# Deeper gather buffers for a third of the run, and paired column blends, in a deformable convolution with experts

## The chip, the cores and the metric

The kernel runs on one core of a Trainium2 chip. The core has a matrix engine (PE; its weight loads are shown apart as PEld), a vector engine (DVE), a scalar engine (ACT), a GpSimd engine (POOL) and a SyncE queue (SP) that only issues transfers. All transfers run on 16 DMA engines that the queues share. Each engine takes its instructions in the order of its own queue and waits on semaphores for the others. The metric is the device time of one execution in microseconds; the time before is the median of three runs.

## The reference

The input is four images of 256 channels and 64 x 64 positions. Each is normalised over its channels and goes through three modulated deformable 3 x 3 convolutions with ReLU. A plain convolution gives, for each position and each of nine taps, an offset (dy, dx) and a mask; the image is sampled there bilinearly, and the samples are multiplied by the tap's 256 x 256 weights:

```python
om = conv(x, w_off) + b_off                  # 27 channels: 9 x (dy, dx), 9 masks
sampled = _bilinear(x, ys, xs) * mask[:, None]
out = jnp.einsum('bikhw,oik->bohw', sampled, wk) + b[None, :, None, None]
```

The result is added to the input. Then each of the 16384 tokens (256 values) is normalised, a gate picks two of eight experts, and each expert is a layer 256 to 512 with GELU and a layer 512 to 256, weighted by the gate and added. All is float32.

## The kernel before

**Stages and blocks.** The convolution work is cut into twelve stages, one per layer and image, in the order (0,0), (1,0), (0,1), (2,0), (1,1), (0,2), (2,1), (1,2), (0,3), (2,2), (1,3), (2,3), given as (layer, image). The document numbers them 0 to 11. Image 0 leaves its last layer with stage 3; the experts of an image run beside later stages, so the first expert work falls in stage 4. A stage has 8 blocks of 512 positions, a block 9 taps, and a tap 4 tiles of 128 positions: 288 tiles a stage, 3456 in all. Tiles are handled in pairs (`t0` is 0 or 2).

**A tile.** The image lies in DRAM as a table whose row holds a position and the one below it, 512 floats. One gather (POOL, L503) brings for each of 128 positions two neighbouring rows of the table (left and right column), 4 KB, into a buffer `g` of the pool `gat` (ten buffers, 512 KB each). The *column blend* (DVE, L509) mixes the upper and the lower value in each of the two columns, in place, 128 x 512 values. The *row blend* (DVE, L514) mixes the left and the right column into a sample `s` of the pool `smp` (eight buffers), 128 x 256 values; with it the gather's buffer is free. ACT multiplies the sample by its mask (L517). PE transposes the two halves of the sample into `tp` (L532); ACT copies the `tp` of a pair into `sT` (L535); the sample buffers are free after the transposes. When a tap has its two pairs, PE multiplies `sT` by the tap's weights into `acc` (L555): four products of 128 x 512.

**Order.** `samples` puts out a pair's gathers, blends and scalings; `turn` puts out the transposes and copy of the pair that came LAG = 2 pairs earlier; `finish` puts out the products of the tap before. That is the order in the program. A planner then fixes the queue of each engine from a priority, the buffers it believes free and its own estimate of durations, so a change in one engine's order can change another's. Where the code wants an order it says so with `self.after(x)`: what is put out under it comes behind `x` on its engine. `self.last` holds the latest row blend, and the smaller DVE work is put behind it: the plans of positions and weights (`off_block`, L395 to L427, one per block, behind products L357 and L371), the norm of an image to come (`pre_block`), the tokens (`tokens`).

**The experts.** From stage 4 on, lanes paced by the tap counter put out the routing (`route`, `invert`), the expert steps (`expert`: gather of weights and of 256 tokens, transposes `ftp`, copy `fzT`, products `ph` L856, GELU `hT`, products `py` L874) and the weighted sums (`combine`). Their buffers are the pools `ffn`, `rt` and `gyp`, which in the kernel before are there from the start.

## Time and profile before

| what | value |
| --- | --- |
| median of the runs | 7486.86 us (7480.8, 7486.86, 7520.67) |
| profiled execution, its own time | 7520.62 us |
| its span, first to last instruction | 7518.9 us |
| mean granted TensorE clock | 0.944 |
| transfers | 2223.73 MB, mean 296 GB/s |
| of them gathers and other software transfers | 1947.35 MB |

Stretches from the first gather of a stage to that of the next, in us, with busy time of the engines and busy share of DMA:

| stage | from | long | PE | DVE | ACT | POOL | DMA |
| --- | --- | --- | --- | --- | --- | --- | --- |
| 0 | 93.40 | 558.40 | 487.89 | 406.38 | 254.00 | 310.02 | 0.88 |
| 1 | 651.80 | 466.50 | 388.29 | 340.60 | 215.10 | 306.30 | 0.93 |
| 2 | 1118.30 | 478.80 | 411.43 | 347.38 | 226.49 | 307.18 | 0.92 |
| 3 | 1597.10 | 498.00 | 435.22 | 421.44 | 250.57 | 315.71 | 0.96 |
| 4 | 2095.10 | 543.70 | 480.26 | 401.78 | 250.68 | 345.56 | 0.90 |
| 7 | 3820.00 | 634.30 | 533.11 | 422.88 | 266.36 | 407.76 | 0.85 |
| 10 | 5625.30 | 765.80 | 656.77 | 445.31 | 307.43 | 451.10 | 0.78 |

How to read the profile: a group's line gives code line, engine, operation, output and inputs, shapes and count; then busy time and the mean of one in ns; then the idle time of the engine just before these instructions and what ended it. The chain is followed back from the last instruction: at each step to what released it, or to the instruction before it on its engine; only what is on it set the end. A matmul's end is modelled, so PE's busy time holds some waiting. A line of the timeline gives start, length, engine, code line, operation, shapes, how many in a row, and in brackets the idle time before and who ended it.

### The profile page before, as it was taken

Reading aid. Unit: us, or ns where it says so; the run is one execution under the profiler, and the core shown is the slowest. Engines: PE = TensorE matmul, PEld = TensorE weight load, DVE = VectorE, ACT = ScalarE, POOL = GpSimd, SP = SyncE. Lnnn points to the kernel's source line nnn. Section 1 sums busy time; section 2 is a strip of 40 time slices with the busy share of each in tenths; the row PEclk is TensorE's granted clock in tenths of the full one; section 3 lists DMA queues with packets and bytes.
Section 4 is the critical chain, followed back from the end, with each engine's and each line's share of the span. In section 5 each row is a group of like instructions: output and inputs, shape, how many; then the busy total and the mean of one; then the engine's idle time right before and its main releaser. Section 6 shows DMA issues by size and latency. Waiting matters only on the chain.

```text
span 7518.9 us, 88985 instructions
## 1 busy us (share of the span) xinstructions
PE 6443.2 (86%) x26500; PEld 3618.8 (48%) x26500; DVE 4952.9 (66%) x11467; ACT 3266.0 (43%) x7141; POOL 4476.5 (60%) x4245
## 2 busy tenths in 40 slices
PE   6898888888898888889988888888888788977887
PEld 3443333334454444445554445444544555644565
DVE  6776777768887666567777556666768554667421
ACT  3444544445544444445443434444444333444322
POOL 4654666656666565556557656555656565666543
PEclk8999999999999999999999999999999899989998
DMA  8997999989998888888888888888888777888644
GB/s 266 337 325 274 352 342 335 346 331 356 362 349 311 300 305 297 278 315 322 314 293 316 293 280 314 295 302 294 308 306 299 251 271 240 288 302 287 211 139 123
DMA packets 800320, 2223.73 MB, mean 296 GB/s; under 512 B 104729, under 2 KB 302873, under 8 KB 794081
## 3 DMA queue, kind: packets, MB, share of 16 engines
q0 software_dynamic: 551200, 1947.35, 73.3%
q1 hardware_dynamic: 248640, 270.69, 10.9%
q8 instruction: 215, 3.52, 0.2%
q14 instruction: 265, 2.16, 0.1%
HBM read 2160.68 MB, written 196.40 MB: 313 GB/s over the span
## 4 chain that ended last, share of the span: by engine, by line
PE 69%; ACT 10%; issue 7%; another core or an unknown queue 6%; DVE 4%; DMA 2%; POOL 1%; SPq 0%; ACTq 0%; DVEq 0%; POOLq 0%
PE acc L555 34%; PE tp L532 10%; PE ph L856 7%; PE py L874 6%; PE po L357 6%; ACT sT L535 4%; ACT s L517 3%; DVE g L509 2%; DVE s L514 1%; PE pm L371 1%; ACT hT L866 1%; PE ftp L840 1%; ACT win L577 1%; PE tpv L325 1%
## 5 line engine op out<-in xcount | busy, mean ns | idle before, releaser
L503 POOL DMA_INDIRECT g<-tab,idx x3456 | 3685.4, 1066 | 2371.6 <-DVE s L514 1061.8
L555 PE MATMUL acc<-sT,wk 128*128 128x512 f32 x6912 | 3492.1, 620 | 253.4 <-ACT sT L535 147.5
L509 DVE SCALAR_TENSOR_TENSOR g<-g,cf 128x512 f32<-128x512 f32 x3456 | 2559.2, 742 | 269.1 <-DMA g<-tab,idx 245.5
L514 DVE SCALAR_TENSOR_TENSOR s<-g,cf 128x256 f32<-128x256 f32 x3456 | 1662.7, 483 | 1331.3 <-PE tp L532 729.9
L535 ACT COPY sT<-tp 128x512 f32<-128x512 f32 x1728 | 1002.0, 585 | 2312.0 <-PE tp L532 1553.0
L517 ACT ACTIVATE s<-s,cf 128x256 f32<-128x256 f32 x3456 | 1629.5, 508 | 256.7 <-DVE s L514 160.7
L555 PEld LDWEIGHTS acc<-sT,wk 128*128 128x128 f32 x6912 | 1198.9, 198 | 1106.7 <-issue 816.7
L532 PEld LDWEIGHTS tp<-ident,s 128*128 128x128 f32 x6912 | 893.2, 146 | 1666.2 <-issue 898.9
L532 PE MATMUL tp<-ident,s 128*128 128x128 f32 x6912 | 1287.3, 286 | 439.2 <-ACT s L517 253.8
L856 PE MATMUL ph<-fzT,w 128*128 128x256 f32 x2608 | 720.8, 411 | 78.0 <-ACT fzT L844 28.1
L874 PE MATMUL py<-w,hT 128*128 128x256 f32 x2608 | 671.1, 396 | 103.5 <-ACT hT L866 58.0
L856 PEld LDWEIGHTS ph<-fzT,w 128*128 128x128 f32 x2608 | 506.3, 205 | 212.9 <-issue 69.6
L874 PEld LDWEIGHTS py<-w,hT 128*128 128x128 f32 x2608 | 484.5, 196 | 242.0 <-issue 91.9
L866 ACT ACTIVATE hT<-ph,w 128x256 f32<-128x256 f32 x652 | 281.9, 471 | 616.3 <-PE ph L856 378.2
L812 POOL DMA_INDIRECT zt<-z,tok x326 | 333.8, 1024 | 161.5 <-issue 88.0
L800 POOL DMA_INDIRECT w<-in_W,wrow x163 | 178.0, 1092 | 381.2 <-issue 138.8
L357 PE MATMUL po<-win,wo 128*32 128x504 f32 (+1 forms) x2304 | 366.0, 615 | 6.5 <-ACT win L301 4.2
L892 DVE TENSOR_TENSOR y<-py,w 128x512 f32<-128x512 f32 x163 | 111.9, 686 | 341.5 <-PE py L874 285.1
L915 POOL DMA_INDIRECT gy<-ys,slots x256 | 255.6, 998 | 104.5 <-issue 70.0
L930 DVE SCALAR_TENSOR_TENSOR ta<-gy,cw,ta 128x256 f32<-128x256 f32 x256 | 120.6, 480 | 125.6 <-DMA gy<-ys,slots 78.4
L357 PE MATMUL po<-win_pre,wo 128*32 128x504 f32 (+1 forms) x1152 | 184.2, 617 | 2.0 <-ACT om L366 2.0
L366 ACT ACTIVATE om<-po,bo 128x512 f32<-128x512 f32 x96 | 65.9, 687 | 265.3 <-PE po L357 156.3
(154 smaller groups left out, 2961.0 us busy)
## 6 DMA issues: line engine op xcount, KB each, us to landing
tab<-hv SPq DMA_DIRECT2D x512, 128.0 KB
g<-tab,idx POOLq DMA_INDIRECT x3456
ys<-y SPq DMA_DIRECT2D x163, 256.0 KB
tab<-h_pre SPq DMA_DIRECT2D x128, 256.0 KB
wk<-in_conv_w SPq DMA_DIRECT2D x99, 256.0 KB
xc_pre<-in_x SPq DMA_DIRECT2D x32, 512.0 KB
xr_tok<-in_x SPq DMA_DIRECT2D x32, 512.0 KB
t<-t_tok SPq DMA_DIRECT2D x32, 512.0 KB
```

Source lines behind the costliest of these rows:

```text
L357: nc.tensor.matmul(po[g * Q : (g + 1) * Q, :].rearrange("q (r w) -> q r w", w=W)[:, :, x0:x1], lhsT=self.wo[l][:, 3 * ky + kx, c, :], rhs= ...
L503: self.gathered = nc.gpsimd.indirect_dma_start(out=g.rearrange("p x s f -> p (x s f)"), out_offset=None, in_=self.table(*self.stages[i]), ...
L509: nc.vector.scalar_tensor_tensor(g[:, :, 0, :], g[:, :, 1, :], cf[:, j, 0:1], g[:, :, 0, :], ALU.mult, ALU.add,)
L514: self.last = nc.vector.scalar_tensor_tensor(s, g[:, 1, 0, :], cf[:, j, 1:2], g[:, 0, 0, :], ALU.mult, ALU.add)
L517: nc.scalar.activation(s, s, AF.Copy, scale=cf[:, j, 2:3])
L532: self.turned = nc.tensor.transpose(tp[:, c, u * P : (u + 1) * P], ss[u][:, c * P : (c + 1) * P], self.ident)
L535: nc.scalar.copy(self.sT[:, :, t0 * P : (t0 + 2) * P], tp)
L555: nc.tensor.matmul(acc[:, o, :], lhsT=self.wk[k][:, c, o * P : (o + 1) * P], rhs=sT[:, c, :], start=(k == 0 and c == 0), stop=(k == K - 1 ...
L812: self.nc.gpsimd.indirect_dma_start(out=zt, out_offset=None, in_=grp.zd, in_offset=bass.IndirectOffsetOnAxis(ap=grp.tok[:, j : j + 1], axi ...
L856: nc.tensor.matmul(ph[:, h, :], lhsT=w1[:, o : o + P], rhs=zT[:, c, :], start=(c == 0), stop=(c == CC - 1),)
L866: nc.scalar.activation(ht[:, h, :], ph[:, h, :], AF.Gelu, bias=w1[:, k : k + 1])
L874: nc.tensor.matmul(py[:, u, :], lhsT=hT[h // 2][:, h % 2, u * P : (u + 1) * P], rhs=w2[:, h * C : (h + 1) * C], start=(h == 0), stop=(h == ...
```

## The change

For stages 0 to 3 two more pools, `gatx` and `smpx`, of eight buffers each stand beside `gat` and `smp`; gathers and samples go round over 18 and 16 buffers in place of 10 and 8. The pools `ffn`, `rt` and `gyp` are no longer made at the start. When stage 4 begins, `late_pools` gives the two extra pools back, makes the three expert pools in their place, and gathers and samples go on with 10 and 8.

In `samples`, a pair's two column blends now come first and its two row blends after them; `self.after(newest)` holds both row blends behind the second column blend. In the kernel before, each tile's row blend came right after its own column blend.

```diff
--- before.py
+++ after.py
@@ -36,6 +36,8 @@
 FT = 1 << FT_LOG
 FU = FT // P
 GB = 10
+GS = 8
+GX = 8
 LAG = 2
 LEAST = 2.0**-30
 WINN = CC * (RPB + 2) * W
@@ -138,13 +140,19 @@
         self.wt = pool("wt", 2)
         self.small = pool("small", 1)
         self.big = pool("big", 2)
-        self.ffn = pool("ffn", 2)
-        self.rt = pool("rt", 1)
         self.rt2 = pool("rt2", 2)
-        self.gyp = pool("gyp", 4)
         self.smT = pool("smT", 2)
-        self.smp = pool("smp", 8)
+        self.smp = pool("smp", GS)
         self.gat = pool("gat", GB)
+        self.pool = pool
+        self.early = ctx.enter_context(ExitStack())
+        more = [
+            self.early.enter_context(tc.tile_pool(name=name, bufs=GX))
+            for name in ("gatx", "smpx")
+        ]
+        self.gats = [self.gat] * GB + [more[0]] * GX
+        self.smps = [self.smp] * GS + [more[1]] * GX
+        self.drawn = 0
         self.ps = pool("ps", 3, space=bass.MemoryType.PSUM)
         self.ps1 = pool("ps1", 1, space=bass.MemoryType.PSUM)
 
@@ -479,6 +487,14 @@
         )
         self.wk[k] = wk
 
+    def late_pools(self):
+
+        self.early.close()
+        self.gats, self.smps = [self.gat], [self.smp]
+        self.ffn = self.pool("ffn", 2)
+        self.rt = self.pool("rt", 1)
+        self.gyp = self.pool("gyp", 4)
+
     def main_block(self, i, n, wins):
         l, b = self.stages[i]
         plan = self.plans.pop((l, b, n))
@@ -496,24 +512,32 @@
 
         nc = self.nc
         idx, cf = plan
-        ss = []
+        ss, gs = [], []
         for t in (t0, t0 + 1):
             j = t * K + k
-            g = self.gat.tile([P, 2, 2, C], F32, tag="g", name=f"g_{i}_{n}_{j}")
+            g = self.gats[(self.drawn + len(gs)) % len(self.gats)].tile(
+                [P, 2, 2, C], F32, tag="g", name=f"g_{i}_{n}_{j}"
+            )
             self.gathered = nc.gpsimd.indirect_dma_start(
                 out=g.rearrange("p x s f -> p (x s f)"),
                 out_offset=None,
                 in_=self.table(*self.stages[i]),
                 in_offset=bass.IndirectOffsetOnAxis(ap=idx[:, j : j + 1], axis=0),
             )
-            nc.vector.scalar_tensor_tensor(
+            newest = nc.vector.scalar_tensor_tensor(
                 g[:, :, 0, :], g[:, :, 1, :], cf[:, j, 0:1], g[:, :, 0, :],
                 ALU.mult, ALU.add,
             )
-            s = self.smp.tile([P, C], F32, tag="s", name=f"s_{i}_{n}_{j}")
-            self.last = nc.vector.scalar_tensor_tensor(
-                s, g[:, 1, 0, :], cf[:, j, 1:2], g[:, 0, 0, :], ALU.mult, ALU.add
-            )
+            gs.append((j, g))
+        for j, g in gs:
+            s = self.smps[self.drawn % len(self.smps)].tile(
+                [P, C], F32, tag="s", name=f"s_{i}_{n}_{j}"
+            )
+            self.drawn += 1
+            with self.after(newest):
+                self.last = nc.vector.scalar_tensor_tensor(
+                    s, g[:, 1, 0, :], cf[:, j, 1:2], g[:, 0, 0, :], ALU.mult, ALU.add
+                )
             nc.scalar.activation(s, s, AF.Copy, scale=cf[:, j, 2:3])
             ss.append(s)
         return ss
@@ -1071,6 +1095,8 @@
         self.ffn_constants()
         for i, (l, b) in enumerate(self.stages):
             wins, pre = {}, {}
+            if self.stages[i - 1] == (NL - 1, 0):
+                self.late_pools()
             for n in range(NB):
                 for gen in self.later[:2]:
                     self.aside(6, gen, True)
```

## The prediction

> **What bounds the kernel now.** I read the page's busy times and chain first, then the waits of the first four stages (the only ones that get the new buffers), then one tap in the timeline, then the two blends.
>
> ```profile
> PE 6443.2 (86%) x26500; PEld 3618.8 (48%) x26500; DVE 4952.9 (66%) x11467; ACT 3266.0 (43%) x7141; POOL 4476.5 (60%) x4245
> PE 69%; ACT 10%; issue 7%; another core or an unknown queue 6%; DVE 4%; DMA 2%; POOL 1%; SPq 0%; ACTq 0%; DVEq 0%; POOLq 0%
> PE acc L555 34%; PE tp L532 10%; PE ph L856 7%; PE py L874 6%; PE po L357 6%; ACT sT L535 4%; ACT s L517 3%; DVE g L509 2%; DVE s L514 1%; PE pm L371 1%; ACT hT L866 1%; PE ftp L840 1%; ACT win L577 1%; PE tpv L325 1%
> ...
> L509 DVE SCALAR_TENSOR_TENSOR g<-g,cf 128x512 f32<-128x512 f32 x3456 | 2559.2, 742 | 269.1 <-DMA g<-tab,idx 245.5
> L514 DVE SCALAR_TENSOR_TENSOR s<-g,cf 128x256 f32<-128x256 f32 x3456 | 1662.7, 483 | 1331.3 <-PE tp L532 729.9
> ```
>
> PE and the ACT work tied to it make 79% of the chain; VectorE has 4%, DMA and GpSimd 3% together. So a faster VectorE or an earlier gather can shorten only a small part. The waits from 93.4 to 2095 us, where there is no expert work (columns: total us, times, longest):
>
> ```profile
> ACT sT L535 <- PE tp L532: 609.8, 380, 5.7
> ...
> POOL g L503 <- DVE s L514: 292.1, 262, 10.9
> ...
> DVE s L514 <- PE tp L532: 198.0, 252, 4.9
> ...
> ACT s L517 <- DVE s L514: 45.8, 40, 10.4
> ...
> DVE g L509 <- DMA g<-tab,idx: 13.2, 4, 10.9
> ```
>
> The 292 and 198 us are what a lack of buffers looks like: GpSimd waits for a gather buffer, VectorE for a sample buffer that PE has not turned yet. But they are waits of engines that are ahead. VectorE waited for a gather only 13.2 us, and ACT for a sample only 45.8 us, of 2002. What sets the pace there is seen in one tap:
>
> ```profile
> 902.67 0.38 PE L532 MATMUL tp<-ident,s 128*128 128x128 f32 x2
> ...
> 903.14 0.59 ACT L535 COPY sT<-tp 128x512 f32<-128x512 f32 x1 [2.62 <-PE tp L532]
> ...
> 903.62 0.91 ACT L517 ACTIVATE s<-s,cf 128x256 f32<-128x256 f32 x2
> ...
> 904.19 0.83 PE L532 MATMUL tp<-ident,s 128*128 128x128 f32 x4 [0.28 <-ACT s L517]
> ...
> 905.06 0.58 ACT L535 COPY sT<-tp 128x512 f32<-128x512 f32 x1 [0.53 <-PE tp L532]
> ...
> 905.70 1.12 PE L555 MATMUL acc<-sT,wk 128*128 128x512 f32 x2 [0.68 <-ACT sT L535]
> ```
>
> ACT holds the copy of one pair ahead of the scaling of the next, idles 2.62 us for PE, then copies and scales, and PE waits in turn: a loop of PE and ACT. It is set by the order of the two queues. More sample buffers do not let ACT past its copy.
>
> **The change, part by part.** Each number is a change to the profiled execution of 7520.6 us (span 7518.9 and 1.7 around it). That execution lies 33.8 us (0.45%) above the median of the runs shown, 7486.9; the sum is carried to the median unscaled.
>
> *Column blends ahead of row blends.* No instruction is added or removed; the VectorE queue is reordered, the GpSimd queue is the same instruction by instruction, SyncE's has three loads of tokens (ta) later and three others swapped with a neighbour. What VectorE gains is in its timeline, first the old order, then a place where the old kernel already had two columns and two rows together:
>
> ```profile
> 900.47 0.75 DVE L509 SCALAR_TENSOR_TENSOR g<-g,cf 128x512 f32<-128x512 f32 x1
> 901.35 0.48 DVE L514 SCALAR_TENSOR_TENSOR s<-g,cf 128x256 f32<-128x256 f32 x1
> 901.76 0.74 DVE L509 SCALAR_TENSOR_TENSOR g<-g,cf 128x512 f32<-128x512 f32 x1
> ...
> 3940.20 1.41 DVE L509 SCALAR_TENSOR_TENSOR g<-g,cf 128x512 f32<-128x512 f32 x2
> 3941.53 0.88 DVE L514 SCALAR_TENSOR_TENSOR s<-g,cf 128x256 f32<-128x256 f32 x2
> 3942.32 1.41 DVE L509 SCALAR_TENSOR_TENSOR g<-g,cf 128x512 f32<-128x512 f32 x2
> ```
>
> Column to its own row: 901.35-900.47 = 0.88 us from start to start; row to the next column: 0.41. A pair is 2 x 1.29 = 2.58. Together, two columns take 3941.53-3940.20 = 1.33 and two rows 3942.32-3941.53 = 0.79: 2.12 a pair. That is 0.46 x 1728 pairs = 795 us off VectorE's queue.
> How much is on the path? The page gives the two blends 2% and 1% of the chain (1.6% and 1.2% unrounded), 2.8% of 7519 = 210 us. A pair is 2 x (0.742+0.483) = 2.45 us busy, so at most 210 x 0.46/2.45 = 39 us goes, and less where another chain is close behind or where a pair already stands together. Bounds: 0, and all of ACT's idle time before L517 that a blend ended, 160.7 (whole run) + 23.9 = 185 us. I take -30, near the chain's figure, since the chain is the row that weighs a wait by what follows it.
> [...]
>
> *Eight more buffers of each kind, stages 0 to 3.* They take away up to 292 us of GpSimd's and 198 us of VectorE's waiting. Cover: gathers already land about ten tiles early (13.2 us of waiting). If the cover counted for nothing and every wait of ACT for a row blend went, 45.8 us; at the other end 0, or a loss if eighteen gathers in flight press on other transfers (below). Some of the 45.8 is already in the 30 above: I take -10.
> [...]
>
> *PE's order.* The new VectorE order changes what the planner thinks is ready, and it writes another PE queue. Before, a tap's products stood between the transposes of tile one and two; now the two tiles' transposes mostly stand together. That alone is neutral: the second tile's transposes start after the same work. Two counts in the queues matter. (a) Taps whose first product has under 0.85 us of other PE work behind the transposes whose copy it needs (the time from the transposes' issue to the product above): 305 of 864 before, 378 after, 73 more. Waits of this kind, and of the next, over the whole run:
>
> ```profile
> DVE g L509 <- DMA g<-tab,idx: 245.5, 90, 10.9
> ...
> PE acc L555 <- ACT sT L535: 147.5, 171, 5.5
> ...
> PEld ph L856 <- ACT fzT L844: 47.7, 68, 3.4
> ```
>
> 147.5/171 = 0.86 us each, 63 us for 73 as the upper end; many are covered in part, and at the 0.55 us or so that the placement leaves on average I take +40. Lower end 0. (b) First products of an expert step (ph) with under 0.85 us of work behind their own transposes (ftp): 67 of 163 before, 14 after. 47.7/68 = 0.70 us each, 37 us for 53; at 0.5, since PE had other work under part of it, -26. Lower gain 0. The other hops (tile to tile, om to pm) keep their counts within 5 us.
>
> *Waits that the pairing adds.* Row one now waits for column two, so for gather two. VectorE waited for a gather 90 times in the run; behind such a late gather the pair now has column, row, row (0.66+0.40+0.48) in place of column, row (0.88+0.48): 0.2 to 0.3 us more, 27 us if all of it were on the path. Queued behind row one are ACT's scaling of both tiles and PE's transposes, and gather buffer one is freed one column (0.66 us) later. DMA has 2% of the chain: +5, between 0 and 27.
>
> *The pools' change-over before stage 4.* By then the rotation has come round evenly (1152 tiles, over 18 and over 16), so the gathers just fall back to ten ahead. The expert pools' first use is after that; their first three loads on SyncE come some fifty rows later in its queue, long before the sums that need them. 0.
>
> Sum: -30 -10 +40 -26 +5 = **-21 us**, 7466.
>
> **The rivals.**
> *VectorE was the real bound.* For: in stages 3 and 4 (1597 to 2639 us) its blends alone are about 8% of the chain, and the time from a row blend to its transposes often falls to 1.1 us there. If all that ACT waited for blends goes and (b) is full: -185 x 0.5 (half of ACT's waits reaching PE) - 37 = about -130, 7357; the middle of this case, with half of that beside the sum, 7410. Against: elsewhere VectorE is blocked by PE 730 us in total, so it is ahead.
> *PE's order costs more than it gives (the other side).* 73 taps more wait at 0.86, and (b) gains little because expert steps have other waits: +63, with nothing from VectorE +60, 7550. It decides as soon as (a) exceeds the VectorE and expert gains together, 66 us at my figures, so only where one of these fails too.
> *Traffic.* Eighteen gathers of 512 KB ahead in stages 0 to 3, where DMA is already busy 0.88 to 0.96 of the time, delay table stores and what the chain calls an unknown queue (6%, some 490 us). For: that share is large and unexplained. Against: consumption, not issue, sets the rate of gathers. A tenth more of it is +49: 7535.
> *The blends don't speed up* (start to start stays 0.88): only 30 us are lost from the sum, 7496, no change.
>
> **How the numbers follow.** A change under 0.5% (37 us) is about what a measurement of this kernel can't tell from none. No change, the forecast: 0.36, 7466, own range 7450 to 7524. VectorE the bound: 0.34. PE's order: 0.19. Traffic: 0.11. So faster 0.34, same 0.36, slower 0.30. The range takes in the first two rivals to where their bounds add: low -39-46-37 = -122, 7365; high +63+27 = +90, 7577.
>
> **What would show it.** Right: VectorE's start-to-start from column to column 0.66 and its busy time nearly unchanged while its waits grow; POOL g <- DVE s and DVE s <- PE tp far smaller before 2095 us, with stages 1 and 2 still 460 to 485 us each; PE acc <- ACT sT up from 147.5 towards 190; ph <- ACT fzT nearly gone. Wrong: stages 0 to 2 shorter by over 20 us each (the buffers mattered), the DVE share of the chain falling by over 100 us in stages 3 to 11, or the unknown queue's share moving by more than a point.

## The result, and the profile after

The changed kernel takes 7890.8 us (median of 4, 7871.6 to 7958.0), the kernel before 7492.0 (4 runs): **1.053 times as long, 95% interval 1.048 to 1.058**. The forecast was no change, 7466, in a range that ended at 7577. The profiled execution took 7907.3 us (span 7905.6), 386.7 more than the one of before.

Cut at the first transposes of each stage, stages 0 to 3, which have the new buffers, went from 2015.5 to 2385.5 us (+370). Stages 4 to 10, which have the new order with the old buffers, went from 4294.6 to 4287.7. So the whole loss of this execution lies where both parts of the change are present. Within stages 0 to 3, PE idles 303 us more (274 to 577) and is busy 67 us longer (1742 to 1809) for the same work.

From the page of the changed kernel (busy times; chain by engine and by line; the gather and the column blend):

```profile
PE 6503.6 (82%) x26500; PEld 3664.7 (46%) x26500; DVE 4802.0 (61%) x11467; ACT 3255.6 (41%) x7141; POOL 4991.9 (63%) x4245
...
PE 62%; another core or an unknown queue 12%; ACT 10%; issue 8%; DVE 4%; DMA 3%; POOL 2%; SPq 0%; ACTq 0%; POOLq 0%; DVEq 0%
...
L521 POOL DMA_INDIRECT g<-tab,idx x3456 | 4135.4, 1197 | 2267.2 <-DVE s L538 1077.0
...
L527 DVE SCALAR_TENSOR_TENSOR g<-g,cf 128x512 f32<-128x512 f32 x3456 | 2489.2, 743 | 638.6 <-DMA g<-tab,idx 561.9
```

The column blend itself is as long as before (743 ns in the mean, 742 before). What grew is the share of the unknown queue, from 6% to 12% of a longer span, and the gather on GpSimd, from 1066 to 1197 ns in the mean. The waits from 91.4 to 2450 us, the stages 0 to 3 of this run (total us, times, longest):

```profile
POOL g L521 <- DVE s L538: 385.8, 177, 20.0
...
ACT sT L559 <- remote: 219.1, 33, 24.5
...
DVE g L527 <- DMA g<-tab,idx: 99.8, 78, 10.3
...
DVE s L538 <- PE tp L556: 70.3, 47, 4.7
```

VectorE's wait for a sample buffer fell from 198 to 70 us, as the buffers should make it. But GpSimd waits more, not less (292 to 386), VectorE now waits for gathers (13 to 100), and another row has grown: ScalarE's copy waits 219 us for something that the profile calls remote, up to 24.5 us at a time. Before, from 91 to 2095 us, it was:

```profile
ACT sT L535 <- remote: 53.7, 12, 10.6
```

The same 500 us of the two kernels (columns: busy us and instruction count of PE, PEld, DVE, ACT, POOL; then granted PE clock, DMA share, GB/s), before and after:

```profile
600.00:1100.00 500.00, 422.95 (x1688) 190.40 (x1683) 356.92 (x741) 229.01 (x507) 302.82 (x285) 0.97 0.89 321
```

```profile
600.00:1100.00 500.00, 367.07 (x1437) 163.25 (x1434) 284.43 (x652) 187.00 (x416) 288.61 (x229) 0.88 0.75 268
```

Every engine does less in the same time, GpSimd takes longer for each of its instructions (1.26 us of busy time for 1.06), and the granted clock falls from 0.97 to 0.88. The clock record of the run is made of windows at 1.0 and at 0.5; those at 0.5 sum to 166 us in stages 0 to 3 before and to 487 after. PE's work in a window at 0.5 takes longer (an `acc` product 1061 ns in the median there and 592 elsewhere, by the profile's modelled ends), so the 67 us of longer busy time can come from there.

**First finding: gathers are held off.** The changed kernel's timeline around one gather:

```profile
1013.47 16.63 POOL L521 DMA_INDIRECT g<-tab,idx  x1 [0.30 <-issue]
...
1027.88 1.41 DVE L527 SCALAR_TENSOR_TENSOR g<-g,cf 128x512 f32<-128x512 f32 x2
...
1029.70 0.88 DVE L538 SCALAR_TENSOR_TENSOR s<-g,cf 128x256 f32<-128x256 f32 x2 [0.41 <-PE tp L556]
...
1030.41 0.99 POOL L521 DMA_INDIRECT g<-tab,idx  x1 [0.30 <-DVE s L538]
...
1031.70 0.94 POOL L521 DMA_INDIRECT g<-tab,idx  x1 [0.30 <-issue]
```

A gather that usually takes 1 us takes 16.63. VectorE runs columns and rows without any gap all this time; its first gap is from 1029.29 to 1029.70, where it has used up its sample buffers, and the gather ends at 1030.10. Then one gather follows another every 1.3 us. Over the trace, 142 of the 4201 gathers (the experts' counted in) took over 2 us, 756 us together, the longest 17.4; before it was 25 (68 us, 3.8). Of the 142, 84 have a gap of VectorE within them, and 80 of these end 0.8 to 0.9 us after the first such gap begins (0.82 in the median). In the old order each row blend waited for its own column blend, which left 0.13 us of gap twice in a pair. The pairing removes both.

A gap is not the only thing that lets a gather through. Of the other 58, 36 end 0.83 to 0.99 us after VectorE starts an instruction with at most one tensor input in SBUF, without any gap. In the same run's timeline, where VectorE takes the tokens' statistics between two blends (L64), the gather ends at 2095.02, 0.90 us after they start:

```profile
2088.18 6.84 POOL L521 DMA_INDIRECT g<-tab,idx  x1 [0.30 <-issue]
...
2094.12 0.41 DVE L64 BATCH_NORM_STATS2 st_tok<-t_tok 128x6 f32<-128x256 f32 x1
```

The time from the first gap to the gather's end does not grow with the length of the hold: it is 0.82 us for the shortest of the 84 (2.20 us) as for the longest two (16.63 and 17.43). So in this trace a gather is kept out and then let through, and not slowed in step with VectorE; the one of 1013.47 is kept out over some thirty instructions in a row.

**Second finding: what is called remote is PE.** ScalarE's copy waits for PE's semaphore and its own, no other core runs, and in the trace the update of PE's semaphore is recorded just ahead of the copy's start, many microseconds after the modelled end of the transposes that make it. I call such a signal late when the recorded update comes over 2 us after the modelled end of the last PE instruction that updates the semaphore. From 100 to 2100 us late signals sum to 143 us before (39 of them, longest 9.4) and to 886 us after (94, longest 21.9). Not all updates are recorded, so these are sizes and not exact sums. In the 10 us ahead of a late signal the DMA moved 401 GB/s in the median before and 409 after, against 336 and 279 over the whole stretch.

### The profile page after: what moved, and what is told of

It is laid out like the page before. It is cut to its first block, busy times and chain, and to the rows that moved or that the text cites. A ratio compares the mean times of both kernels' runs of the same rounds, so it can differ in the third digit from the quotient of the medians.

```text
span 7905.6 us, 88514 instructions
## 1 busy us (share of the span) xinstructions
PE 6503.6 (82%) x26500; PEld 3664.7 (46%) x26500; DVE 4802.0 (61%) x11467; ACT 3255.6 (41%) x7141; POOL 4991.9 (63%) x4245
## 4 chain that ended last, share of the span: by engine, by line
PE 62%; another core or an unknown queue 12%; ACT 10%; issue 8%; DVE 4%; DMA 3%; POOL 2%; SPq 0%; ACTq 0%; POOLq 0%; DVEq 0%
PE acc L579 31%; PE tp L556 9%; PE py L898 6%; PE ph L880 6%; PE po L365 5%; ACT sT L559 4%; ACT s L541 3%; DMA g<-tab,idx 2%; DVE g L527 1%; PE pm L379 1%; PE ftp L864 1%; PE tpv L333 1%; POOL gy L939 1%; DVE s L538 1%
## 5 line engine op out<-in xcount | busy, mean ns | idle before, releaser
L521 POOL DMA_INDIRECT g<-tab,idx x3456 | 4135.4, 1197 | 2267.2 <-DVE s L538 1077.0
L579 PE MATMUL acc<-sT,wk 128*128 128x512 f32 x6912 | 3477.3, 628 | 375.4 <-ACT sT L559 181.4
L527 DVE SCALAR_TENSOR_TENSOR g<-g,cf 128x512 f32<-128x512 f32 x3456 | 2489.2, 743 | 638.6 <-DMA g<-tab,idx 561.9
L538 DVE SCALAR_TENSOR_TENSOR s<-g,cf 128x256 f32<-128x256 f32 x3456 | 1538.8, 478 | 926.0 <-PE tp L556 534.7
L579 PEld LDWEIGHTS acc<-sT,wk 128*128 128x128 f32 x6912 | 1248.2, 200 | 1486.8 <-issue 1162.4
L556 PE MATMUL tp<-ident,s 128*128 128x128 f32 x6912 | 1181.3, 287 | 574.7 <-ACT s L541 292.8
L541 ACT ACTIVATE s<-s,cf 128x256 f32<-128x256 f32 x3456 | 1569.3, 506 | 178.9 <-DVE s L538 134.7
L556 PEld LDWEIGHTS tp<-ident,s 128*128 128x128 f32 x6912 | 850.8, 146 | 1444.6 <-issue 694.8
L880 PE MATMUL ph<-fzT,w 128*128 128x256 f32 x2608 | 691.4, 404 | 67.0 <-ACT fzT L868 27.4
L836 POOL DMA_INDIRECT zt<-z,tok x326 | 373.5, 1146 | 160.1 <-issue 89.7
L403 DVE TENSOR_TENSOR pos<-pos,base 128x72 f32<-128x72 f32 x96 | 21.9, 228 | 435.6 <-ACT pos L399 418.7
L379 PE MATMUL pm<-strips,om 128*128 128x27 f32 x768 | 108.5, 282 | 142.8 <-ACT om L374 123.5
```

Of the source, the lines that this page charges most:

```text
L521: self.gathered = nc.gpsimd.indirect_dma_start(out=g.rearrange("p x s f -> p (x s f)"), out_offset=None, in_=self.table(*self.stages[i]), ...
L527: newest = nc.vector.scalar_tensor_tensor(g[:, :, 0, :], g[:, :, 1, :], cf[:, j, 0:1], g[:, :, 0, :], ALU.mult, ALU.add,)
L538: self.last = nc.vector.scalar_tensor_tensor(s, g[:, 1, 0, :], cf[:, j, 1:2], g[:, 0, 0, :], ALU.mult, ALU.add)
L541: nc.scalar.activation(s, s, AF.Copy, scale=cf[:, j, 2:3])
L556: self.turned = nc.tensor.transpose(tp[:, c, u * P : (u + 1) * P], ss[u][:, c * P : (c + 1) * P], self.ident)
L579: nc.tensor.matmul(acc[:, o, :], lhsT=self.wk[k][:, c, o * P : (o + 1) * P], rhs=sT[:, c, :], start=(k == 0 and c == 0), stop=(k == K - 1 ...
```

## The experiments

The theory at the start was **A, hold-off**: VectorE's gapless runs keep gathers from being issued, and deep sample buffers make those runs long. Rivals: **B, traffic**, eighteen gathers ahead press on other transfers; **C, the order** itself, the new queues of PE and VectorE.

### Each part alone

**pair_alone**: the new order, old buffers. Every engine's queue is that of the changed kernel, instruction by instruction; on SyncE three loads of tokens stand elsewhere.

```diff
-            for name in ("gatx", "smpx")
+            for name in ()
...
-        self.gats = [self.gat] * GB + [more[0]] * GX
-        self.smps = [self.smp] * GS + [more[1]] * GX
+        self.gats = [self.gat]
+        self.smps = [self.smp]
```

> The pairing without the new buffers (10 gather and 8 sample buffers all the way; every queue is the same as after, instruction by instruction). Theory A, hold-off: a gather cannot get through GpSimd while VectorE runs its blends without a gap, and only deep sample buffers let VectorE run that long; so this kernel loses little: 7490, between 7450 and 7530, stages 0 to 3 within 15 us of before each, fewer than 60 gathers over 2 us. Rival B, traffic: eighteen gathers in flight are the whole loss, so this also gives 7490. Rival C, the new order itself (PE's queue and VectorE's) is the loss and the buffers only happen to be in the same stages: 7850 to 7900.

Measured: 7576.7, ratio 1.013 [1.008, 1.017]. 135 gathers over 2 us, the longest 9.8: the hold-off is there without the new buffers too, more often than the 60 expected, and the time lies above the 7530 that theory A allowed.

**buf_alone**: the new buffers, old order. Every engine's queue is that of the kernel before, but for the same three loads on SyncE.

```diff
         for t in (t0, t0 + 1):
...
-            gs.append((j, g))
-        for j, g in gs:
             s = self.smps[self.drawn % len(self.smps)].tile(
```

> The new buffers without the pairing (18 gather and 16 sample buffers in stages 0 to 3, queues in the old order, each row blend behind its own column blend). Theory A, hold-off: the dependent row blend leaves 0.13 us of VectorE idle after each column, gathers slip in there; fewer than 40 gathers over 2 us, and 7490 (7440 to 7530). Rival B, traffic (18 gathers ahead press on table stores, loads and the unknown queue): 7800 or more, stages 0 to 3 some 90 us longer each. Rival C, the order: 7490.

Measured: 7742.8, 1.035 [1.031, 1.040]. Only 27 gathers over 2 us, as theory A said, and still 251 us slower, which it did not. So A alone falls: the buffers' loss does not come from held-off gathers. The two parts give 85 and 251 us; together 399, which is 63 more than their sum.

A stall of this kernel in its timeline:

```profile
786.42 0.38 PE L553 MATMUL tp<-ident,s 128*128 128x128 f32 x2
...
792.73 0.75 DVE L527 SCALAR_TENSOR_TENSOR g<-g,cf 128x512 f32<-128x512 f32 x1
793.25 1.04 POOL L521 DMA_INDIRECT g<-tab,idx  x1 [0.31 <-issue]
797.98 0.59 ACT L556 COPY sT<-tp 128x512 f32<-128x512 f32 x1 [15.54 <-remote]
797.98 0.48 DVE L535 SCALAR_TENSOR_TENSOR s<-g,cf 128x256 f32<-128x256 f32 x1 [4.51 <-remote]
...
799.02 1.12 PE L553 MATMUL tp<-ident,s 128*128 128x128 f32 x4 [11.36 <-ACT s L538]
```

The transposes of 786.42 are done by 786.80 in the model; PE's signal is recorded at 797.90, and in the same instant ScalarE and VectorE, which both wait for it, start. Until 794.3 GpSimd had issued a gather every 1.28 us. Instruction loading does not explain it: of 68 gaps of PE over 3 us from 100 to 6800 us of this trace, 7 have a transfer of the instruction queues that ends within 2.5 us ahead of their end.

**swap_rows**: the changed kernel, only the two row blends of a pair exchanged. The row blend that comes first now needs the column blend just ahead of it, and waits for it: one break in each pair.

```diff
-        for j, g in gs:
+        for j, g in gs[::-1]:
...
-            ss.append(s)
+            ss.insert(0, s)
```

> The changed kernel with all its buffers, and only the two row blends of a pair exchanged: the second tile's row blend comes first, straight behind the column blend that it needs. That leaves one short idle gap of VectorE (about 0.13 us) in each pair, and costs VectorE 0.22 us a pair. Theory A, hold-off: gathers get through once in each pair, the gathers over 2 us fall from 142 to under 50, and the time to 7450 to 7530. Rival B, traffic: buffers and gathers ahead are as after, so 7850 to 7900. Rival C, the order: PE's queue is nearly that of after, 7850 to 7900.

Measured: 7383.9, 0.987 [0.982, 0.991], faster than both kernels and below what A expected. 12 gathers over 2 us. 507 us lie between this and the changed kernel, with the same buffers. The planner's PE queue moved too, in some 3100 of 26500 places, so this run does not separate the break from PE's new order.

**gat10_smp16**: the pairing with ten gather and sixteen sample buffers.

```diff
-            for name in ("gatx", "smpx")
+            for name in ("smpx",)
...
-        self.gats = [self.gat] * GB + [more[0]] * GX
-        self.smps = [self.smp] * GS + [more[1]] * GX
+        self.gats = [self.gat]
+        self.smps = [self.smp] * GS + [more[0]] * GX
```

> The pairing with sixteen sample buffers but only ten gather buffers in stages 0 to 3. Theory A, hold-off: VectorE can blend every gather that has landed without a gap, but there are at most ten of them, about 10.6 us of blends, so gathers over 2 us stay many (70 to 140) but none is longer than some 11 us; 7600 to 7850. Rival B, traffic: at most ten gathers ahead as before, so 7490. Rival C, the order: 7850 to 7900.

Measured: 7778.8, 1.040 [1.035, 1.045], 151 gathers over 2 us, longest 10.9: as A said. The same buffers in the old order come to 1.032 (smp16_alone, below), so most of this loss is not the pairing's.

### Which buffer, and which order

**pair_swap**: swap_rows without extra buffers.

```diff
-            for name in ("gatx", "smpx")
+            for name in ()
...
-        self.gats = [self.gat] * GB + [more[0]] * GX
-        self.smps = [self.smp] * GS + [more[1]] * GX
+        self.gats = [self.gat]
+        self.smps = [self.smp]
```

> The exchanged row blends with the old 10 gather and 8 sample buffers all the way (swap_rows without its extra buffers; every queue is the same as there). In swap_rows the stages 4 to 10, which have the old buffers, were 155 us shorter than before (4139 for 4295), stages 0 to 3, which have the new ones, 12 us. Theory A (a gap of VectorE in each pair keeps gathers going, and then deep buffers do no harm): 7360 to 7410, stages 0 to 3 within 15 us each of swap_rows. Theory B (deep buffers always cost, and hide a part of the gain of the new order in stages 0 to 3): those stages 15 to 20 us shorter each than in swap_rows, 7300 to 7340.

Measured: 7331.3, 0.977 [0.975, 0.980]. The time is the one that theory B gave: deep buffers cost something here too. Stages 0 to 3 take 1965.0 us, with the new buffers 2003.6, some 10 us a stage for the 15 to 20 expected; the two ran on different chips (before 7505 and 7491), so a part of the 53 us may be the chips'.

**smp16_alone** and **gat18_alone**: old order (the edit of buf_alone), and one kind of buffer each.

```diff
-        self.gats = [self.gat] * GB + [more[0]] * GX
-        self.smps = [self.smp] * GS + [more[1]] * GX
+        self.gats = [self.gat]
+        self.smps = [self.smp] * GS + [more[0]] * GX
...
```

```diff
-        self.smps = [self.smp] * GS + [more[1]] * GX
+        self.smps = [self.smp]
...
```

> Old order of the blends, queues as before, 10 gather buffers, and sixteen sample buffers in stages 0 to 3. With both sets of buffers this order lost 251 us although only 27 gathers took over 2 us, so that loss isn't the hold-off. If it is VectorE's running ahead (it stops at steps that wait for PE, and then catches up in one stretch of back-to-back gathers), sample buffers alone give most of it: 7640 to 7760. If it is the number of gathers ahead: 7490.

> Old order, queues as before, eighteen gather buffers and the old eight sample buffers. VectorE can run no further ahead than before. If the running ahead is the cause: 7470 to 7510. If the number of gathers ahead is: 7640 to 7760.

Measured: 7746.1, 1.032 [1.030, 1.035], and 7535.8, 1.003 [1.001, 1.005]. The sample buffers make most of the loss, not the gathers ahead. Waits of the two, from 91 to 2200 us with sixteen sample buffers, and from 91 to 2150 us with eighteen gather buffers:

```profile
ACT sT L556 <- remote: 239.5, 41, 12.0
DVE pos L403 <- ACT pos L399: 232.7, 23, 18.2
```

```profile
DVE pos L403 <- ACT pos L399: 66.5, 10, 20.9
ACT sT L556 <- remote: 61.3, 10, 16.9
```

With eight sample buffers `pos` costs VectorE 55 to 67 us (55 before), with sixteen 233: VectorE runs further ahead and then stands at a step in its queue that needs PE's latest work. What the eight more buffers buy is a longer wait at that place and a longer run to catch up behind it. The wait is not itself the loss: on a chip without late signals (below) it is 128 us with sixteen, and the kernel no slower.

### Is it the saturated DMA?

**pace_buf**: buf_alone with a useless memset of 128x128 on GpSimd ahead of each gather.

```diff
+            nc.gpsimd.memset(self.idle, 0.0)
             self.gathered = nc.gpsimd.indirect_dma_start(
```

> Both sets of new buffers in the old order, with a useless memset of 128x128 on GpSimd ahead of each gather (about 0.2 us in the profile's first rows), so that gathers can come at most every 1.45 to 1.55 us and no longer every 1.25. In 100 to 2100 us PE's signals that came over 2 us after the modelled end of the work behind them add up to 143 us before, 307 with the buffers alone, 886 with both parts, and in the 10 us ahead of them the DMA moved 398 to 410 GB/s against 280 to 340 on average. If the saturated DMA of back-to-back gathers is what holds PE up, the pace keeps it under 360 GB/s and the loss of 251 us goes: 7450 to 7560. If the gathers' rate has nothing to do with it, the memsets only add work: 7740 to 7900. The planner's queues differ somewhat from those without the memset.

Measured: 7783.6, 1.038 [1.035, 1.041]. The run decides nothing: back-to-back gathers went from 1.25 to 1.34 us, not to 1.5, and late signals still came at 410 GB/s (314 us of them).

**pace_more**: the same with a longer memset.

```diff
-        self.idle = self.small.tile([P, 128], F32, tag="idle", name="idle")
+        self.idle = self.small.tile([P, 384], F32, tag="idle", name="idle")
```

> The same test as pace_buf with a longer memset (128x384), since there the gathers still came every 1.34 us in a row and the DMA still reached 410 GB/s ahead of PE's late signals. With some 1.5 us from gather to gather the DMA can move at most 350 GB/s of gathers. If the saturated DMA is what holds PE's signals up: late signals in 100 to 2100 us fall from 314 us to under 100, the time to 7500 to 7620 (the gathers' own rate begins to limit: a stage needs one every 1.65 us). If it isn't: 7780 to 7950.

Here the surprise came from the other side. On the chip of this run the kernel *before* takes 6807 us, and in none of the traces of that chip is there a late signal in the first 2100 us. The paced kernel took 7608.5, 1.118 [1.116, 1.120]: without late signals the pace is pure loss. Repeated on another chip:

> Both sets of new buffers, old order, and a memset of 128x384 on GpSimd ahead of each gather. On a chip without late signals of PE it took 7608 us, limited by the gathers' own rate. If late signals need a DMA that is saturated by back-to-back gathers, then on a chip with them (before about 7500) the paced kernel has nearly none and takes about the same, 7590 to 7680, less than the 7743 of the same buffers without the pace. If they don't, it loses there as much as the others do, some 10%: 7900 to 8300. On a chip without them: 7600 to 7620 again.

Measured on a chip whose kernel before takes 7628.7: 7732.3, 1.014 [1.011, 1.018]. Two chips that differ by 12% in the kernel before differ by 1.6% in the paced one. Late signals sum to 87 us, all before 255 us and from 747 to 787 us, where nine to twelve gathers still came in the 15 us ahead; from 2100 to 6800 us they sum to 32, against 793 from 2100 to 6700 in the first profile of before. The two paced runs from 1100 to 1600 us, first the chip without late signals:

```profile
1100.00:1600.00 500.00, 397.55 (x1423) 175.84 (x1422) 321.83 (x630) 209.80 (x457) 398.60 (x531) 0.97 0.85 298
```

```profile
1100.00:1600.00 500.00, 400.89 (x1439) 177.47 (x1437) 320.20 (x636) 209.99 (x459) 389.71 (x519) 0.96 0.83 293
```

There the two chips do the same. So the late signals go with gathers that follow each other closely, and the pace, 1.55 us from gather to gather, takes most of them away. Close gathers alone are not enough: the paced kernel on the other chip also has up to twelve within 15 us, and no late signal. The 7732 lie a little above what was expected (7590 to 7680); the first two stages, where late signals were left, took 92 us longer than on the other chip. The planner's queues differ between the two paces and buf_alone, so only the two runs with the long memset compare directly.

### The same kernels on chips without late signals

**smp6** and **swap_smp6**: before, and pair_swap, with six sample buffers.

```diff
-        self.smp = pool("smp", 8)
+        self.smp = pool("smp", 6)
```

> The kernel before with six sample buffers in place of eight, and nothing else (the planner moves some 760 of 17802 places in PE's queue). If VectorE's running ahead of PE is what costs (sixteen buffers gave +241), then fewer cost less, or VectorE starves PE where it was only just ahead: between 7440 and 7520 by the first, over 7560 by the second.

> The exchanged row blends with ten gather and six sample buffers. If running ahead costs also here: 7290 to 7330, below the 7331 with eight. If eight are needed to cover VectorE's stops: 7350 to 7450.

Measured beside 6807.1: 6830.7, 1.004 [1.003, 1.006], and 6818.1, 1.002 [1.001, 1.003]. Their expectations were for the other kind of chip; here six buffers cost a little.

**after_2**, **smp16_alone_2**, **pair_swap_2**: three kernels again, beside a kernel before of 6803.6.

> The changed kernel once more, because the last call ran on a chip on which the kernel before takes 6807 us and no late signal of PE is to be found in any of the four traces, while on the chips of the two calls before that it takes 7491 and 7505 and late signals add up to 143 us in 100 to 2100 us. On a chip of the first kind: if late signals are what turns held-off gathers and catching up into lost time, the change costs little there, between -40 and +80 us; if holding off the gathers costs by itself, +250 to +400 as before. On a chip of the second kind: 7850 to 7950.

> Sixteen sample buffers in stages 0 to 3 with the old order and ten gather buffers, 241 us slower on the chip where it ran first. On a chip without late signals: within 40 us of before, if they are the cause; again 200 to 260 us slower if running ahead costs by itself. On a chip with them: 200 to 280 us slower, as before.

> The exchanged row blends with the old buffers, 173 us faster than before (2.3%) on the chip where it ran first. On a chip without late signals: it has the same order and gaps, so it stays ahead, but by less: 10 to 80 us faster. On a chip with them: 150 to 200 us faster.

Measured: 6859.4, 1.008 [1.006, 1.009]; 6800.3, 0.999 [0.998, 1.000]; 6795.2, 0.999 [0.998, 1.000]. The change costs 56 us there instead of 399, the sample buffers nothing instead of 241. The gathers are held off as before (141 over 2 us, 611 us together). What VectorE and GpSimd wait for from 91 to 1990 us of the changed kernel on this chip (no row of any engine there says remote):

```profile
DVE g L527 <- DMA g<-tab,idx: 238.5, 292, 11.1
...
POOL g L521 <- DVE s L538: 64.0, 165, 5.1
```

Now VectorE, held up by its own hold-off, waits 239 us for gathers, and PE's idle stretches over 1 us sum to 65 us from 100 to 2100 us, for 375 in the first run. On this chip the DMA is at 390 GB/s or more for longer (1372 us of the 2000 from 100 to 2100, in windows of 2 to 3 us, for some 800 in the first run), and those of PE's idle stretches that begin there sum to about 50 us, against 331 in the first run and 105 in the kernel before. So a saturated DMA by itself costs PE little; on some chips it comes with late signals.

### Is a break in VectorE's run enough?

**pair_gap**: pair_alone with a copy of one column between the second column blend and the first row blend, which has to wait for the former.

```diff
+        self.mark = self.small.tile([P, 1], F32, tag="mark", name="mark")
...
-            newest = nc.vector.scalar_tensor_tensor(
+            nc.vector.scalar_tensor_tensor(
...
+        newest = nc.vector.tensor_copy(self.mark, g[:, 0, 0, 0:1])
         for j, g in gs:
```

> The pairing with the old buffers (pair_alone, 7577), and between the second column blend and the first row blend of each pair one copy of a single column (128x1) on VectorE that reads what the column blend wrote, so it has to wait for it. It puts a gap of VectorE into each pair without exchanging the row blends, and adds 1728 small instructions to VectorE, at 0.06 to 0.2 us each. Hold-off theory: the gathers over 2 us fall from 135 to under 30 and the time to 7330 to 7450, most of the way to the exchanged rows (7331). If instead it is the order in which rows, scalings and transposes come that makes the exchanged rows fast: 7570 to 7650, since this adds work and exchanges nothing.

> The paired order with one small dependent copy between the column and the row blends, old buffers. It was 28 us faster than before on the chip without late signals, with 6 gathers over 2 us. Hold-off theory: on a chip with late signals it comes to 7330 to 7450, level with the exchanged rows within 60 us; if the exchange of the rows is what counts, it stays at 7550 to 7650. On a chip without them: 20 to 40 us faster than before, as measured.

> The pairing with the old buffers and one small dependent copy in each pair, which on chips without late signals of PE is 0.4% faster than before. On a chip with them the pairing without the copy was 1.3% slower and the exchanged rows 2.3% faster than before. If the gap of VectorE is what made the exchanged rows fast there, this kernel is 1.0% to 2.3% faster than before; if the exchange is what counts, it is 0.5% to 2% slower. On a chip without late signals: 0.4% faster again, and this stays open.

Measured on the two chips without late signals: 6779.5, 0.996 [0.995, 0.997], and 6778.0, 0.996 [0.994, 0.998]. On one with them, beside 7651.0: 7491.7, **0.978 [0.975, 0.981]**, level with the exchanged rows (0.977), with 8 gathers over 2 us for the 135 of pair_alone (1.013). The timeline of that run:

```profile
899.92 1.41 DVE L528 SCALAR_TENSOR_TENSOR g<-g,cf 128x512 f32<-128x512 f32 x2
900.13 1.35 POOL L522 DMA_INDIRECT g<-tab,idx  x1 [0.30 <-DVE s L540]
901.36 0.15 DVE L533 COPY mark<-g 128x1 f32<-128x1 f32 x1
901.53 0.88 DVE L540 SCALAR_TENSOR_TENSOR s<-g,cf 128x256 f32<-128x256 f32 x2
```

The gather of 900.13 ends at 901.48, 0.12 us after the copy starts. One more instruction in each pair, 1728 in all, and the kernel stands 2.2% below before on its chip, where pair_alone stood 1.3% above it on another (3.4% between the ratios; the times themselves are 7491.7 and 7576.7, since the two chips differ by 2.1% in the kernel before). The exchange of rows is not needed for it. PE's queue differs from that of pair_alone in some 2400 places, and from that of pair_swap in 3700; what pair_swap and this kernel share against pair_alone is the break. pair_alone never ran on a chip without late signals, so what the break is worth there isn't measured. Whether the copy's wait or its single input lets the gather through, this run does not tell; the changed kernel's own trace has both (a gap, and the token statistics above), and in swap_rows there is only the wait.

### The runs side by side

Late signals: 100 to 2100 us, sum in us. Each ratio is to the kernel before on the same chip: 7491 to 7651 us in the upper ten rows, 6804 to 6807 in the lower. The runs with a memset and with six sample buffers are left out.

| kernel | order | gather / sample buffers | ratio to before | late signals | gathers over 2 us |
|---|---|---|---|---|---|
| pair_swap | paired, break | 10 / 8 | 0.977 | 78 | 12 |
| pair_gap_3 | paired, break | 10 / 8 | 0.978 | 125 | 8 |
| swap_rows | paired, break | 18 / 16 | 0.987 | 154 | 12 |
| before | old | 10 / 8 | 1 | 143 | 25 |
| gat18_alone | old | 18 / 8 | 1.003 | 143 | 26 |
| pair_alone | paired | 10 / 8 | 1.013 | 171 | 135 |
| smp16_alone | old | 10 / 16 | 1.032 | 273 | 26 |
| buf_alone | old | 18 / 16 | 1.035 | 311 | 27 |
| gat10_smp16 | paired | 10 / 16 | 1.040 | 357 | 151 |
| the change | paired | 18 / 16 | 1.053 | 886 | 142 |
| pair_gap, pair_gap_2 | paired, break | 10 / 8 | 0.996 | 0 | 6, 7 |
| pair_swap_2 | paired, break | 10 / 8 | 0.999 | 0 | 17 |
| smp16_alone_2 | old | 10 / 16 | 0.999 | 0 | 23 |
| after_2 | paired | 18 / 16 | 1.008 | 0 | 141 |

Among the upper ten, the ratio goes up with the late signals almost in order (which goes with what, and not which causes which); in the lower rows there are none, and all ratios lie within 1.2% of each other.

## Why the prediction was wrong

- **The buffers' term** ("-10", and "at the other end 0, or a loss if eighteen gathers in flight press on other transfers") is the step that failed. Measured alone: +251 us. The loss named was of the wrong kind: eighteen gathers ahead give +31, sixteen sample buffers +241. The step asked what the removed waits of VectorE and GpSimd were worth, and not what these waits do for others: they pace VectorE, and with it the gathers. That the lost pace is what costs is argued and not shown; what is shown is that late signals of PE grow from 143 to 311 us with the buffers alone, and that on a chip without late signals the sample buffers cost nothing (-3 us), so the step failed by 241 us on one kind of chip only. More buffers alone brought no gain on any chip.
- **The pairing's terms** (-30 for VectorE, +40 and -26 for PE's order, +5 for waits, sum -11) came to +85 with the old buffers. The cadence was right: 663 ns in the median from a column to one right behind it, for the forecast 0.66. PE's order came to nothing in the run with the old buffers: PE's `acc` behind `sT` stayed at 147.3 us (147.5 before, for the forecast +40), and the weight loads of `ph` behind `fzT` at 47.3 (47.7 before, for -26), though their number halved from 68 to 33; in the changed kernel the two rows are 181.4 and 43.1. So both terms were mis-sized, by amounts that nearly cancel. What is missing is a term for the 0.13 us gaps that go. They were written down as VectorE's loss, within the 0.46 us a pair, and not as the times at which a gather gets through between blends. With one break left in, the same pairing gives -173 us on a chip with late signals and -8 to -28 on one without, where the forecast of about no change does hold for this part.
- **The waits of gathers** (+5, at most 27): VectorE's wait for gathers went from 245.5 to 561.9 us over the run; with the pairing alone it is 563.1, with the buffers alone 246.3. It was costed as the pair's coupling, while the gathers themselves came late.
- **The pools' change-over** (0) was right, by stages 4 to 10.
- **The rivals.** "Traffic" had the right side, and the sign to watch for was right: the unknown queue's share moved by six points. Its mechanism (stores and an unknown queue delayed by gathers ahead) is not what was found, and its price, +49, was a guess at a tenth of the queue's share. "PE's order costs more" gave 7550 by another mechanism. None of the cases held a loss above 90 us, so the range ended 314 us below the result. On a chip without late signals the change costs 0.8%, which such a range would have held, though on the side of a loss.
- **What was to be seen.** "POOL g <- DVE s far smaller" failed (292 to 386 us): the engine that got more buffers waits longer for them. On a chip without late signals the same kernel has this row at 64 us, with as many gathers held off, so held-off gathers alone do not make it grow. "Stages 1 and 2 still 460 to 485" failed (572.7 and 570.0).

**What stays open.** Why PE's signal comes late. It comes with gathers close together, and on some chips and not on others. In stages 0 to 3 the DMA runs near 410 GB/s ahead of it, in the later stages of before at 342 in the median. A saturated DMA alone is not enough: pair_swap has the DMA over 400 GB/s in 26% of the time from 100 to 2100 us and 78 us of late signals, before in 20% and 143. Also open is why deep sample buffers and gapless runs make them more. A reading that fits, but was only argued: a late signal stops PE and ScalarE, while VectorE and GpSimd go on until the sample buffers are full, and only then does the DMA drain and the signal arrive (as in the stall shown, where VectorE stopped at 793.5, the last gather was issued at 794.3 and the signal came at 797.9); eight more buffers are eight more gathers, 10 us at the 1.28 us of that stall, until then. One candidate for the cause was not tested, though the traces give it weight: the recording itself. Every execution here was recorded. In the eight traces from the two faster chips at least 99.8% of PE's updates are in the record; in the twelve traces from the others 76 to 84%, and of VectorE's 64 to 83%. So late signals, the longer times and an incomplete record come together on the same chips (on the faster two a whole run has at most two late signals, 9 us); which of them is the cause is open. No run here shows whether the recording holds PE up, or what an unrecorded run would take; if it does, a large part of the 399 us is not the kernel's own.

## What to carry to other kernels

Ask of every wait that a change removes what it gives to other engines: an engine that is ahead and stops now and then also paces the transfers it triggers, and lets the engine next to it through. When GpSimd gathers beside VectorE, keep a short break in each group of VectorE's two-input instructions, by ordering a dependent one straight behind its source or by a small instruction with one input; here that made 2.2% of gain out of 1.3% of loss, on chips with late signals, and the gathers over 2 us fell from 135 (pair_alone) to 12 (pair_swap) and 8 (pair_gap_3), each on another chip. That a stop now and then paces the transfers is argued from these runs, and not shown by one of its own. Before a loss is explained, run the kernel on more than one chip, and see whether the record is complete: the same change cost 5.3% on a chip where a fifth of PE's updates is missing, and 0.8% on one where nearly none is.

## What the runs showed of the hardware

- A gather on GpSimd can be held off while VectorE runs blends with two SBUF inputs without a break: up to 17.4 us, 142 gathers over 2 us in the run of the changed kernel. With a gap of VectorE in it, it ends 0.82 us after the gap begins (80 of 84 within 0.8 to 0.9); without one, mostly 0.83 to 0.99 us after an instruction with at most one tensor input in SBUF starts (36 of 58).
- Chips differ: the same kernel before takes 6804 to 6807 us on two of them and 7491 to 7651 on four others, and the DMA's best 5 us are 422 to 434 GB/s in the traces of both kinds. In the traces of the two, at least 99.8% of PE's semaphore updates are recorded, in those of the others 76 to 84%.
- On the latter, PE's semaphore updates are recorded up to 21.9 us after the modelled end of the work, with nine to twelve gathers in the 15 us ahead as a rule. The profile calls the release remote, though the semaphore is that of the same core's PE.
- The granted clock is 0.5 in windows of 3.4 to 50 us (trace of the changed kernel); in the 7 us ahead of one in its first 2450 us PE idled 3.3 us in the median, against 0.95 elsewhere. They sum to 487 us in stages 0 to 3 of the changed kernel, to 71 us in the same kernel on a chip without late signals.
